# Third layer of a position-bias network: from tiles of eight keys by sixteen sums to tiles of sixteen keys by eight sums

## The chip, the cores and the metric

The kernel runs on one core of a Trainium2 chip. A core has a matrix engine (TensorE, in the profile PE, its weight loads PEld), a vector engine (VectorE, DVE), a scalar engine (ScalarE, ACT), GpSimd (POOL), a queue for transfers (SyncE, SP) and 16 DMA engines. The metric is the device time of one execution in microseconds.

## What is computed

A transformer-like block with deformable attention, followed by a plain attention block. The part that matters here is the bias that is added to the attention logits of the first block. For each of 16 groups (2 images, 8 heads) there are 1024 queries and 64 sampled keys, and each pair of query and key goes through a small network with 128 hidden channels:

```python
pos = grid_q[:, :, None, :] - grid_kv[:, None, :, :]
bias = jnp.sign(pos) * jnp.log1p(jnp.abs(pos))
bias = jax.nn.relu(bias @ cpb_w1 + cpb_b1)     # 2 -> 128
bias = jax.nn.relu(bias @ cpb_w2 + cpb_b2)     # 128 -> 128
bias = (bias @ cpb_w3 + cpb_b3)                # 128 -> 1
sim = jnp.einsum('bhid,bhjd->bhij', qh, kh) + bias
attn = jax.nn.softmax(sim, axis=-1)
```

All data is float32.

## The kernel before

The bias network is a loop of 256 steps (`for s in range(NS)`): 16 groups times 16 steps, each step with 4 keys and all 1024 queries. In one step:

- **Layer 1** (`st_layer1`, L612, VectorE): one instruction adds a table over x and a table over y and clips at zero; the result `h1` has 128 hidden channels on the partitions and 4096 columns. There are three buffers of `h1`, and the step s writes that of step s + 2.
- **Layer 2** (`st_layer2`, L629, TensorE): for each of four blocks z of 32 output channels, eight matmuls of 512 columns. The four keys go to four column groups of the array, so that a PSUM tile has partition 32 * key + lane, and two banks for the two halves of the queries. ScalarE evicts each block with the rectifier (L636 for z = 0 and 2 into `rx`, L638 for z = 1 and 3, with a scale).
- **The third layer's sum over 128 channels** is made in parts. Block 0 is multiplied by its weights and added to block 1 (`st_sum(s, 0)`, L646, VectorE); likewise block 2 to block 3 (`st_sum(s, 2)`). Then GpSimd issues a DMA that adds the second result onto the first one (L648). So each key has 32 lanes left. The weights of block 1 and 3 are taken into the eviction, which works because the channels are ordered by the sign of their weight (`rank`, `order`, `arrange`, once at the start): a "bound" block may hold only channels whose sign fits its place.
- **Folding of lanes.** For a pair of steps s and s + 1 (s even), `st_fold` adds the odd lanes of tile s onto its even lanes (L660, a DMA with accumulation from GpSimd, 64 partitions). `st_join` copies the odd lanes of tile s + 1 to the odd lanes of tile s (L663, SP), and then adds the even lanes of s + 1 there (L665, GpSimd). Tile s then holds 8 keys, each with 16 sums.
- **Layer 3** (`st_layer3`, L694, TensorE) takes two such tiles every four steps: four matmuls of 512 columns with 32 output rows (two halves of the queries, two tiles), which sum 16 lanes for each of 8 keys and put them in their rows of the logits in PSUM (`sims`). The weights `w3f` are zeros with a mask of signs inside; a slice of it moves the result to the right rows. The last four steps of all are taken apart, unfolded, with `w3u`. For each pair of heads `st_layer3` also starts the product of queries and keys (L678).

Buffers of the results: `ua` (4) for even steps, `uo` (2) for odd ones, `ub` (3) for the second sums, `rx` (3).

Beside the loop run, one piece a step, the preparation of later groups (`later`: `chain` for queries and offsets, `sample` for keys and values) and the softmax of finished groups (`softmax_steps`). The order on each engine is that of the program, moved in places by `issue_after`, which puts an instruction behind a given one of its engine. `chain` loads the input rows `xn` and multiplies them with `wq`; `sample` builds interpolation weights `wt` and multiplies the sampled keys with `wk`. `wq` and `wk` lie together in the tile `ws`.

After the loop follow the output projection (L874), the MLP (L927) and the second attention (L1058, L1156).

Of the kernel before, what the change touches and what calls it, by code (L numbers as in the profile page):

```python
# [8 lines left out]
F32 = mybir.dt.float32  # L9
AF = mybir.ActivationFunctionType  # L10
# [36 lines left out]
def conv_seq_kernel(ctx: ExitStack, tc: tile.TileContext, x, xt, kst, pst, cst, vec, wsm, outw, w1, w2, wl, wlt, brow, out):  # L47
# [22 lines left out]
    w3f = cp.tile([P, 56], F32, name="w3f")  # L70
# [70 lines left out]
    with tc.tile_pool(name="lp", bufs=2) as lp:  # L141
# [21 lines left out]
        ws = ph.tile([P, 1408], F32, name="ws")  # L163
        wq, wk = ws[:, 0:512], ws[:, 512:1024]
        pw = [ws[:, 1024 + 128 * i : 1152 + 128 * i] for i in range(3)]
        wv = sx.rearrange("p a f j -> p (a f j)")[:, 0:512]
        ow_s = vp[:, 0:NCH, :]
        nc.scalar.dma_start(out=ws[:, 0:P], in_=wsm[:, 0:P])
# [5 lines left out]
        nc.scalar.dma_start(out=ws[:, 1024:1408], in_=wsm[:, 1536:1920])  # L174
# [4 lines left out]
        def load(b, k):  # L179
            xn = ph.tile([P, HW], F32, name="xn")  # L180
            nc.sync.dma_start(out=xn, in_=xv[:, k, b, :])
            return xn

        xn0 = [load(0, 0)]
# [13 lines left out]
        w2t, crow, tri, four, chan, mask = (  # L198
            pz[:, a:b] for a, b in ((0, 128), (128, 256), (256, 384), (384, 400), (400, 401), (401, 413))
        )  # L200
        wb = vs[:, VOFF["w3"] : VOFF["w3"] + 2]
        po_, rn, t4, pc, dc, k16, one = (
            pw_[:, a:b] for a, b in ((0, 1), (1, 3), (3, 4), (4, 5), (5, 6), (8, 24), (128, 256))
# [15 lines left out]
        def order():  # L219
            nc.vector.tensor_scalar(k16, four, rn[:, 1:2], 4.0, ALU.is_le, ALU.mult)  # L220
            nc.vector.tensor_reduce(t4, k16, AX.X, ALU.add)
            free, bound = ([t.rearrange("p (a b l) -> p b a l", a=2, b=2)[:, i] for t in (place, crow)] for i in (0, 1))
            nc.vector.tensor_scalar(bound[0], bound[1], t4, 64.0, ALU.is_ge, ALU.mult)
            nc.vector.tensor_tensor(bound[0], bound[0], bound[1], ALU.add)
            nc.vector.tensor_scalar(free[0], free[1], t4, None, ALU.add)
            nc.vector.tensor_scalar(perm, place, pc, None, ALU.is_equal)

        def arrange():
            nc.gpsimd.memset(prod, 0.0)
            ps = simp.tile([P, 512], F32, name="sim")  # L230
            nc.tensor.matmul(ps[:, 0:P], w2t, perm, start=True, stop=True)
            for z in range(4):
                for u in range(4):
                    nc.tensor.matmul(
                        ps[32 * u : 32 * u + 32, P + 2 * z : P + 2 * z + 2], perm[:, 32 * z : 32 * z + 32], wb,
                        start=True, stop=True,
                    )
            nc.scalar.copy(cw2, ps[:, 0:P])
            nc.scalar.copy(
                sc[:, 0:8].rearrange("p (a z) -> p z a", a=2), ps[:, P : P + 8].rearrange("p (z a) -> p z a", a=2)  # L240
            )
            nc.gpsimd.tensor_scalar(sc[:, 8:9], sc[:, 1:2], 0.0, 2.0, ALU.is_ge, ALU.mult)
            nc.gpsimd.tensor_scalar(sc[:, 8:9], sc[:, 8:9], 1.0, None, ALU.subtract)
            nc.gpsimd.tensor_scalar(sc[:, 0:4], sc[:, 0:4], sc[:, 8:9], None, ALU.mult)
            for z in (1, 3):
                nc.gpsimd.tensor_tensor(sc[:, 4 + z : 5 + z], sc[:, 4 + z : 5 + z], sc[:, z : z + 1], ALU.mult)
            nc.gpsimd.tensor_scalar(w3f[:, 24:32], mask[:, 0:8], sc[:, 8:9], None, ALU.mult)
            nc.gpsimd.tensor_scalar(w3u[:, 28:32], mask[:, 8:12], sc[:, 8:9], None, ALU.mult)
# [7 lines left out]
        def chain(ci):  # L256
# [3 lines left out]
            for i in range(K):  # L260
                k = k0 + i
                if i == 0:
                    xn = xn0.pop()
                nc.scalar.activation(xn, xn, AF.Identity, bias=col("bn1b", k), scale=bns[:, k : k + 1])
                if ci > 0:
                    yield
                ps = flat("psq")

                for f_, h_, f, h in QUADS:
                    nc.tensor.matmul(  # L270
                        ps[h_, f * 512 : (f + 1) * 512], wq[f_, k * P + 64 * f : k * P + 64 * f + 64],
                        xn[f_, h * 512 : (h + 1) * 512], start=True, stop=True,
                    )
                for f_, h_, f, h in QUADS:
                    copy = nc.vector.tensor_copy if ci == 0 and f == 1 else nc.scalar.copy
                    copy(qa[f_, b, k, h * 512 : (h + 1) * 512], ps[h_, f * 512 : (f + 1) * 512])
                if i + 1 < K:
                    xn = load(b, k + 1)
                elif ci + 1 < len(CHAINS):
                    xn0.append(load(*CHAINS[ci + 1][0]))  # L280
                yield
# [132 lines left out]
        def sample(ci):  # L414
# [23 lines left out]
            for i, (b, k) in enumerate(G):  # L438
# [3 lines left out]
                wt = ph.tile([P, 8, 2, J], F32, name="wt")  # L442
# [10 lines left out]
                for f in range(2):  # L453
                    r, v = slice(64 * f, 64 * f + 64), sg[:, 4, f, i * J : (i + 1) * J]
                    nc.scalar.activation(
                        uv[r].rearrange(rowwise, e=2, t=8), v[r].rearrange(natural, e=2, t=8), AF.Copy,
                        scale=col("bn1b", k)[r],
                    )
# [6 lines left out]
                for t in range(8):  # L465
# [6 lines left out]
                    kv.rearrange(rowwise, e=2, t=8), ps[:, 0:J].rearrange(natural, e=2, t=8), AF.Copy,  # L472
                    scale=bns[:, k : k + 1],
                )
                nc.vector.tensor_tensor(kv, kv, uv, ALU.add)
                yield
# [3 lines left out]
                nc.tensor.matmul(pk[:, 0:J], wk[:, k * P : (k + 1) * P], kv, start=True, stop=True)  # L480
# [38 lines left out]
        with tc.issue_after(nc.cur_bb.bb.instructions[-1]):  # L519
            nc.sync.dma_start(out=wv, in_=wsm[:, 1024:1536])  # L520
            nc.sync.dma_start(out=ow_s, in_=outw)
            nc.sync.dma_start(out=ws[:, P:1024], in_=wsm[:, P:1024])
# [99 lines left out]
        def st_layer2(s):  # L622
            h1 = h1s.pop(s)
            r = []
            for z in range(4):
# [7 lines left out]
                name, bufs = (("rx", 3), (("ua", 4), ("uo", 2))[s % 2], ("rx", 3), ("ub", 3))[z]  # L633
# [18 lines left out]

        def lanes(s, i):
            return sums[s][1].rearrange("(l e) h n -> l e (h n)", e=2)[:, i]

        def st_fold(s):
            with tc.issue_after(added[0]):
                nc.gpsimd.dma_start(out=lanes(s, 0), in_=lanes(s, 1), accum_op=ALU.add)  # L660

        def st_join(s):
            nc.sync.dma_start(out=lanes(s, 1), in_=lanes(s + 1, 1))  # L663
            with tc.issue_after(added[0]):
                nc.gpsimd.dma_start(out=lanes(s, 1), in_=lanes(s + 1, 0), accum_op=ALU.add)  # L665


        def st_layer3(s):
            gi, i = divmod(s // 4, NSL // 4)
# [3 lines left out]
            if f == 0 and i == NSL // 4 - 1:  # L673

                assert state[chain_of[b, k][0]] is None
                sims[gi + 1] = simp.tile([P, 512], F32, name="sim")
                for f_, h_, o, h in QUADS:
                    nc.tensor.matmul(  # L678
                        sims[gi + o][h_, :], kz[f_, b * NCH + k, :], qa[f_, b, k, h * 512 : (h + 1) * 512],
                        start=(o == 1), stop=False,  # L680
                    )
            w = w3f[:, 24 - 8 * i : 56 - 8 * i]
            parts = [[(w, sums[s + 2 * e][1])] for e in range(2)]
            if s + 4 == NS:

                w = [w3u[:, 28 - 8 * i - 4 * o : 60 - 8 * i - 4 * o] for o in range(2)]
                parts = [[(w[o], sums[s + 2 * e + o][1]) for o in range(2)] for e in range(2)]
                parts[1].append((w[1], sums[s + 3][3]))
            for m in range(len(parts[1])):
                for h in range(2):  # L690
                    for e in range(2):
                        if m < len(parts[e]):
# [3 lines left out]
                                stop=(i == NSL // 4 - 1 and m == len(parts[e]) - 1),  # L696
                            )
            for o in range(4):
                sums.pop(s + o)
# [63 lines left out]
        for s in range(NS):  # L763
# [4 lines left out]
            if s % 2 == 1 and 3 <= s < NS - 1:  # L768
                st_join(s - 3)
            if s % 4 == 0 and s // 4 + 1 < 4 * NG:  # L770
                load_tables(s // 4 + 1)
# [33 lines left out]
            if s % 4 == 3 and s >= 7:  # L805
                st_layer3(s - 7)
                if (s - 3) % NSL == 0:
                    tails.append(softmax_steps(s // NSL - 1))
        st_sum(NS - 1, 2)
        st_layer3(NS - 4)  # L810
# [434 lines left out]
def _order(np):  # L1245
# [4 lines left out]
    place = np.where(z % 2 == 1, 4 * (l // 2) + l % 2 + 2 * (z // 2), 32 * (z // 2) + l)  # L1250
    crow = np.broadcast_to(place, (P, P))
    tri = d[:, None] < d[None, :]
    four = np.broadcast_to(4 * np.arange(1, 17), (P, 16))
    pair = (4 * (d % 2) + d // 32)[:, None] == np.arange(8)
    alone = (d // 32)[:, None] == np.arange(4)
    return np.concatenate([crow, tri, four, d[:, None], pair, alone], axis=1).astype(np.float32)
# [87 lines left out]
```

## Time and profile before

| what | us |
|---|---|
| runs of the kernel (three) | 2674.56, 2674.84, 2682.71; median 2674.84 |
| the profiled execution | 2672.5 |
| its span, first to last instruction | 2670.7 |
| start of the first layer-2 matmul | 37.7 |
| end of the last layer-3 matmul | 1922.8 |
| layer 2 on TensorE (L629) | 1784.8 busy |
| layer 1 on VectorE (L612) | 1131.4 busy, 4.40 each |
| sums on VectorE (L646) | 327.0 + 163.5 + 163.6 busy, 1.28 each |

A group row of the profile names the line, the engine, the operation, the tile written and those read, the shapes, how many instructions there are, their busy time, the mean time of one, and the idle time of the engine just before them with what ended it. One matmul of float32 shows as two records. Records of matmuls that run beside each other in different column groups overlap, so the busy time of a group of matmuls is best read from the starts of the next group. A row of the timeline has the start, the length, the engine, the line, the operation, the tiles, how many instructions were merged, and in brackets the idle time before it with what ended it. For DMAs the rows of issues have the queue that issued them, how many, how many KB each and the median time from issue to landing.

### The profile page before, as it was taken

The page shows a single profiled execution, that of the slowest core. Times are in us where ns is not written, and L with a number is a line of the kernel's source. Part 1 is how long each engine was busy: PE and PEld are TensorE (multiplying, and loading weights), DVE is VectorE, ACT ScalarE, POOL GpSimd, SP SyncE. Part 2 cuts the span into 40 slices and gives each one's busy share as a digit, 9 for nine tenths or more (in the row PEclk, how much of TensorE's full clock was granted, in tenths as well). Part 3 has the DMA queues.
Part 4 walks back from the last instruction along what each step waited for, and adds up shares of the span by engine and source line. Part 5 has one row for each costly group of instructions (what it writes and reads, how often), then busy time and mean ns, then how long its engine had stood idle before and what let it go on. Part 6 is the DMA issues. An engine that isn't in the chain of part 4 may idle for free.

```text
span 2670.7 us, 46906 instructions
## 1 busy us (share of the span) xinstructions
PE 2654.7 (99%) x19596; PEld 959.0 (36%) x19596; DVE 2243.1 (84%) x1329; ACT 1690.1 (63%) x2201; POOL 575.5 (22%) x615
## 2 busy tenths in 40 slices
PE   9999999999999999999999999999999999999999
PEld 3343322332333333333323323333344444446455
DVE  7999999999999899999999999999774484466354
ACT  5787898788878888877777777777621131114041
POOL 1222222222222222222222222222243232000000
PEclk9999999999999999999999999999999999999999
DMA  5766766767666666776777676767631111000000
GB/s 199 152 150 144 164 138 142 160 144 157 147 147 151 155 144 141 145 153 140 148 148 145 150 149 143 152 146 148 160 112 47 47 48 45 3 16 0 32 0 32
DMA packets 96131, 316.67 MB, mean 119 GB/s; under 512 B 17104, under 2 KB 19424, under 8 KB 93232
## 3 DMA queue, kind: packets, MB, share of 16 engines
q0 software_dynamic: 57312, 202.26, 40.7%
q1 hardware_dynamic: 38176, 111.10, 11.7%
q8 instruction: 155, 2.54, 0.4%
q14 instruction: 56, 0.46, 0.0%
q10 hardware_dynamic: 432, 0.31, 0.0%
HBM read 74.28 MB, written 6.55 MB: 30 GB/s over the span
## 4 chain that ended last, share of the span: by engine, by line
PE 84%; DMA 5%; issue 4%; DVE 4%; ACT 2%; POOL 1%; DVEq 0%; SPq 0%; POOLq 0%; ACTq 0%
PE ps L629 53%; PE sw L927 14%; PE sw L1058 9%; DMA ua<-ua 2%; DMA ua<-uo 2%; PE sw L1156 2%; PE sim L694 2%; DVE h L612 1%; PE psg L531 1%; DVE ub L646 1%; PE sw L874 1%; ACT rx L636 0%; POOL ua L665 0%; DVE xs L882 0%; DVE ua L646 0%
## 5 line engine op out<-in xcount | busy, mean ns | idle before, releaser
L629 PE MATMUL ps<-h,cw 128*32 128x512 f32 x16384 | 1784.8, 592 | 1.7 <-ACT rx L636 1.6
L612 DVE CUSTOM_DVE_ANT_1 h<-ta,tb 128x4096 f32<-128x4096 f32 (+1 forms) x257 | 1131.4, 4403 | 45.2 <-PE ps L629 41.3
L629 PEld LDWEIGHTS ps<-h,cw 128*32 128x32 f32 x16384 | 541.1, 110 | 1210.6 <-issue 1155.0
L636 ACT ACTIVATE rx<-ps,sc 128x1024 f32<-128x1024 f32 x512 | 568.6, 1111 | 170.5 <-PE ps L629 144.4
L638 ACT ACTIVATE ub<-ps,sc 128x1024 f32<-128x1024 f32 x256 | 308.4, 1205 | 88.5 <-PE ps L629 88.1
L646 DVE SCALAR_TENSOR_TENSOR ub<-rx,sc,ub 128x1024 f32<-128x1024 f32 x256 | 327.0, 1277 | 5.7 <-ACT ub L638 5.7
L648 POOL DMA_DIRECT2D ua<-ub x128 | 114.8, 897 | 722.6 <-DVE ub L646 685.0
L927 PE MATMUL sw<-xb,w1t 128*128 128x512 f32 x448 | 193.7, 592 | 3.0 <-DVE xs L123 3.0
L927 PE MATMUL sw<-hm,w2t 128*128 128x512 f32 x448 | 193.6, 592 | 0.0
L665 POOL DMA_DIRECT2D ua<-uo x126 | 109.8, 871 | 371.3 <-DMA ua<-uo 364.2
L648 POOL DMA_DIRECT2D uo<-ub x127 | 116.4, 916 | 335.8 <-DVE ub L646 283.0
L638 ACT ACTIVATE ua<-ps,sc 128x1024 f32<-128x1024 f32 x128 | 154.2, 1205 | 54.5 <-PE ps L629 54.2
L638 ACT ACTIVATE uo<-ps,sc 128x1024 f32<-128x1024 f32 x128 | 154.1, 1204 | 49.7 <-PE ps L629 43.7
L646 DVE SCALAR_TENSOR_TENSOR ua<-rx,sc,ua 128x1024 f32<-128x1024 f32 x128 | 163.5, 1278 | 12.8 <-ACT ua L638 12.7
L646 DVE SCALAR_TENSOR_TENSOR uo<-rx,sc,uo 128x1024 f32<-128x1024 f32 x128 | 163.6, 1278 | 7.7 <-ACT uo L638 7.3
L123 DVE TENSOR_TENSOR hm<-hm,sw 128x1024 f32<-128x1024 f32 x56 | 67.6, 1219 | 105.1 <-PE sw L927 104.7
L660 POOL DMA_DIRECT2D ua<-ua x126 | 152.1, 1207 | 1.7 <-issue 1.6
L927 PEld LDWEIGHTS sw<-xb,w1t 128*128 128x128 f32 x448 | 85.0, 190 | 110.5 <-issue 105.0
L936 ACT ACTIVATE hm<-hm,vs 128x512 f32<-128x512 f32 x64 | 42.6, 713 | 129.5 <-DVE hm L123 129.5
L927 PEld LDWEIGHTS sw<-hm,w2t 128*128 128x128 f32 x448 | 85.1, 190 | 107.1 <-issue 106.2
L123 DVE TENSOR_TENSOR xs<-xs,sw 128x1024 f32<-128x1024 f32 (+1 forms) x48 | 55.6, 1171 | 72.9 <-PE sw L1058 36.0
L1058 PE MATMUL sw<-aT,vt 128*128 128x512 f32 x224 | 96.7, 593 | 0.3 <-ACT aT L1138 0.3
(239 smaller groups left out, 1798.2 us busy)
## 6 DMA issues: line engine op xcount, KB each, us to landing
ua<-ub POOLq DMA_DIRECT2D x128, 512.0 KB, 4.9
uo<-ub POOLq DMA_DIRECT2D x127, 512.0 KB, 5.3
fb<-fdr SPq DMA_DIRECT2D x64, 512.0 KB, 5.3
ua<-ua POOLq DMA_DIRECT2D x126, 256.0 KB, 6.5
ua<-uo SPq DMA_DIRECT2D x126, 256.0 KB, 2.7
ua<-uo POOLq DMA_DIRECT2D x126, 256.0 KB, 3.8
w1t<-in_w SPq DMA_DIRECT2D x8, 1024.0 KB, 4.8
w2t<-in_w SPq DMA_DIRECT2D x8, 1024.0 KB, 4.8
```

Source lines behind the costliest of these rows:

```text
L123: nc.vector.tensor_tensor(out, a, b_, op)
L612: nc.vector._custom_dve(TENSOR_ADD_SAT, out=h1[:, y : y + step].rearrange("p y t x -> p (y t x)"), in0=a.unsqueeze(1).to_broadcast([P, ste ...
L629: nc.tensor.matmul(ps[32 * q : 32 * q + 32, h, :], cw2[:, 32 * z : 32 * z + 32], h1[:, 16 * h : 16 * h + 16, q, :], start=True, stop=True,)
L636: nc.scalar.activation(o, ps, AF.Relu, bias=sc[:, 4 + z : 5 + z])
L638: nc.scalar.activation(o, ps, AF.Relu, bias=sc[:, 4 + z : 5 + z], scale=sc[:, z : z + 1])
L646: nc.vector.scalar_tensor_tensor(r[1], r[0], sc[:, z : z + 1], r[1], ALU.mult, ALU.add)
L648: nc.gpsimd.dma_start(out=sums[s][1], in_=sums[s][3], accum_op=ALU.add)
L660: nc.gpsimd.dma_start(out=lanes(s, 0), in_=lanes(s, 1), accum_op=ALU.add)
L665: nc.gpsimd.dma_start(out=lanes(s, 1), in_=lanes(s + 1, 0), accum_op=ALU.add)
L694: nc.tensor.matmul(sims[gi][q : q + 32, :], w_, t[:, h, :], start=(i == 0 and f == 0), stop=(i == NSL // 4 - 1 and m == len(parts[e]) - 1),)
L927: nc.tensor.matmul(ps[:, m, :], w[:, a, k, m * P : (m + 1) * P], x[:, b_, k, :], start=(k == 0), stop=(k == 1),)
L1058: nc.tensor.matmul(ps[:, m, :], w[:, a, k, c + m * P : c + (m + 1) * P], x[b_][:, k, :], start=(k == 0), stop=(k == nk - 1),)
```

## The change

Lanes are folded once more. After `st_join`, tile s (s a multiple of 2) has in partition 4l + 2a + e a sum of step s + e. `st_fold2` (for s a multiple of 4) adds the partitions with a = 1 onto those with a = 0, in two DMAs of 32 partitions (e = 0 and 1). `st_join2` copies the partitions with a = 1 of tile s + 2 to those of tile s, in two copies from SP, and adds the partitions with a = 0 of tile s + 2 there, in two DMAs with accumulation from GpSimd. Tile s then holds 16 keys, each with 8 sums, and layer 3 takes two such tiles every eight steps. The channels are ordered in groups of eight by sign in place of four. The last four steps of all stay unfolded and are taken one after another. Results of steps with s % 4 == 2 get buffers of their own (`uc`, 2).

To make room, `wq` and `wk` are no longer held in whole: a piece of 128 columns is loaded with each `xn` and each `xnt`, and `wt` shares the buffer of `xn`, so that the next chain's `xn` is loaded at the end of `sample`.

```diff
-    w3f = cp.tile([P, 56], F32, name="w3f")
+    w3f = cp.tile([P, 48], F32, name="w3f")
...
-        ws = ph.tile([P, 1408], F32, name="ws")
-        wq, wk = ws[:, 0:512], ws[:, 512:1024]
+        ws = ph.tile([P, 3 * P], F32, name="ws")
...
+        wq0 = ph.tile([P, P], F32, name="wq")
+        nc.scalar.dma_start(out=wq0, in_=wsm[:, 0:P])
...
-        def load(b, k):
+        def load(b, k, wq=None):
             xn = ph.tile([P, HW], F32, name="xn")
             nc.sync.dma_start(out=xn, in_=xv[:, k, b, :])
-            return xn
+            if wq is None:
+                wq = ph.tile([P, P], F32, name="wq")
+                nc.sync.dma_start(out=wq, in_=wsm[:, k * P : k * P + P])
+            return xn, wq
...
-            nc.vector.tensor_scalar(k16, four, rn[:, 1:2], 4.0, ALU.is_le, ALU.mult)
-            nc.vector.tensor_reduce(t4, k16, AX.X, ALU.add)
+            nc.vector.tensor_scalar(k8, eight, rn[:, 1:2], 8.0, ALU.is_le, ALU.mult)
+            nc.vector.tensor_reduce(t8, k8, AX.X, ALU.add)
...
-                    xn = load(b, k + 1)
-                elif ci + 1 < len(CHAINS):
-                    xn0.append(load(*CHAINS[ci + 1][0]))
+                    xn, wq = load(b, k + 1)
...
-                wt = ph.tile([P, 8, 2, J], F32, name="wt")
+                wk = ph.tile([P, P], F32, name="wk")
+                nc.sync.dma_start(out=wk, in_=wsm[:, 512 + k * P : 512 + k * P + P])
+                wt = ph.tile([P, 8, 2, J], F32, tag="xn", name="wt")
...
                 nc.vector.tensor_tensor(kv, kv, uv, ALU.add)
+                if i + 1 == K and ci + 1 < len(CHAINS):
+                    xn0.append(load(*CHAINS[ci + 1][0]))
...
-            nc.sync.dma_start(out=ws[:, P:1024], in_=wsm[:, P:1024])
...
-                name, bufs = (("rx", 3), (("ua", 4), ("uo", 2))[s % 2], ("rx", 3), ("ub", 3))[z]
+                name, bufs = (
+                    ("rx", 3), (("ua", 4), ("uo", 2), ("uc", 2), ("uo", 2))[s % 4], ("rx", 3), ("ub", 3)
+                )[z]
...
+        def twos(s, i):
+            t = sums[s][1].rearrange("(l a e) h n -> l a e (h n)", a=2, e=2)[:, i]
+            return [t[:, e] for e in range(2)]
...
+        def add(out, in_):
+            with tc.issue_after(added[0]):
+                nc.gpsimd.dma_start(out=out, in_=in_, accum_op=ALU.add)
+            added[0] = nc.cur_bb.bb.instructions[-1]
...
+        def st_fold2(s):
+            for o, i in zip(twos(s, 0), twos(s, 1)):
+                add(o, i)
+
+        def st_join2(s):
+            for o, i in zip(twos(s, 1), twos(s + 2, 1)):
+                nc.sync.dma_start(out=o, in_=i)
+            for o, i in zip(twos(s, 1), twos(s + 2, 0)):
+                add(o, i)
...
-            w = w3f[:, 24 - 8 * i : 56 - 8 * i]
-            parts = [[(w, sums[s + 2 * e][1])] for e in range(2)]
-            if s + 4 == NS:
-
-                w = [w3u[:, 28 - 8 * i - 4 * o : 60 - 8 * i - 4 * o] for o in range(2)]
-                parts = [[(w[o], sums[s + 2 * e + o][1]) for o in range(2)] for e in range(2)]
-                parts[1].append((w[1], sums[s + 3][3]))
+            w = w3f[:, 16 - 16 * i : 48 - 16 * i]
+            parts = [[(w, sums[s + 4 * e][1])] for e in range(2)]
+            if s + 8 == NS:
+
+                w = [w3u[:, 28 - 16 * i - 4 * o : 60 - 16 * i - 4 * o] for o in range(4)]
+                parts[1] = [(w[o], sums[s + 4 + o][1]) for o in range(4)]
+                parts[1].append((w[3], sums[s + 7][3]))
+                parts[0] = 4 * [None] + parts[0]
...
+            if s % 4 == 0 and s >= 4:
+                st_fold2(s - 4)
+            if s % 4 == 2 and s >= 6:
+                st_join2(s - 6)
...
-            if s % 4 == 3 and s >= 7:
-                st_layer3(s - 7)
-                if (s - 3) % NSL == 0:
+            if s % 8 == 4 and s >= 12:
+                st_layer3(s - 12)
+                if s % NSL == 4:
                     tails.append(softmax_steps(s // NSL - 1))
         st_sum(NS - 1, 2)
-        st_layer3(NS - 4)
+        st_layer3(NS - 8)
```

## The prediction

> **What bounds the kernel now.** I read the engine totals first, then busy time in stretches of sixteen steps of the main loop, then the timeline around one step. The totals:
>
> ```profile
> span 2670.7 us, 46906 instructions
> ...
> PE 2654.7 (99%) x19596; PEld 959.0 (36%) x19596; DVE 2243.1 (84%) x1329; ACT 1690.1 (63%) x2201; POOL 575.5 (22%) x615
> ...
> L694 PE MATMUL sim<-ua,w3f 128*32 128x512 f32 x504 | 74.4, 595 | 1.2 <-DMA ua<-uo 1.2
> ```
>
> TensorE is busy 99% of the span. That alone proves little (matmul ends are modelled), so I looked for gaps. In a quiet stretch one step's 64 layer-2 records start every 6.87 us (0.43 us per four, which run beside each other in four column groups), and nothing but other matmuls lengthens a step. The third layer is such a lengthening: a step with it takes 7.73 us. The row's 74.4 us overlaps other records, so I take its price from starts. TensorE's timeline, first in the loop, then at its end:
>
> ```profile
> 1687.90 1.04 PE L694 MATMUL sim<-ua,w3f 128*32 128x512 f32 x8
> 1688.76 11.77 PE L629 MATMUL ps<-h,cw 128*32 128x512 f32 x108
> ...
> 1918.70 1.04 PE L694 MATMUL sim<-ua,w3f 128*32 128x512 f32 x8
> 1919.56 1.08 PE L694 MATMUL sim<-ua,w3u 128*32 128x512 f32 x8
> 1920.41 1.08 PE L694 MATMUL sim<-uo,w3u 128*32 128x512 f32 x8
> 1921.80 1.05 PE L694 MATMUL sim<-ub,w3u 128*32 128x512 f32 x4 [0.31 <-DVE ub L646]
> 1922.78 3.70 PE L874 MATMUL sw<-qa,vp 128*128 128x512 f32 x8
> ```
>
> One pass of eight records holds TensorE for 1688.76 - 1687.90 = 0.86 us. A pass with only two of the four column groups (x4) is no shorter, 0.98 us.
>
> VectorE is next. Busy time in stretches of sixteen steps (columns: stretch, length, then PE, PEld, DVE, ACT, POOL, clock, DMA share, GB/s):
>
> ```profile
> 394.20:512.10 117.90, 117.23 (x1092) 35.45 (x1088) 117.90 (x69) 99.49 (x138) 28.09 (x32) 1.00 0.68 144
> ...
> 989.90:1106.00 116.10, 115.52 (x1080) 35.70 (x1076) 116.00 (x68) 98.78 (x132) 27.56 (x31) 1.00 0.67 144
> ...
> 1573.10:1688.80 115.70, 115.70 (x1080) 35.22 (x1076) 109.40 (x50) 86.16 (x99) 27.96 (x32) 1.00 0.70 149
> ```
>
> In the last one VectorE has 6.3 us to spare; in the first it has none. Five of the sixteen stretches have it at 99% or more (158, 394, 635, 752 and 990 us): those where the background work reduces taps and prepares samples.
>
> **What the change removes.** Layer 3 ran in the loop at s = 7, 11, ... 255, 63 times; it will run at s = 12, 20, ... 252, 31 times, with the same four matmuls a time. The last of the 63 is the one at 1918.70, so 62 - 31 = 31 passes go before the tail: 31 x 0.86 = 26.7 us. In the tail the passes from 1918.70 to 1922.78 (4.1 us) become five (four last steps, then the last step's second half beside the tile of s = 248): 5 x 0.86 = 4.3 us; the last sum, done at 1921.74, is not late for the fifth. So 26.7 - 0.2, rounded to **26.4 us** off TensorE.
>
> **What it adds: transfers.** Every four steps: two accumulates (fold2) and two copies with two accumulates (join2), each of 32 partitions, 128 KB. That is 252 issues on GpSimd and 126 on SP. By the rows
>
> ```profile
> ua<-ub POOLq DMA_DIRECT2D x128, 512.0 KB, 4.9
> ...
> ua<-ua POOLq DMA_DIRECT2D x126, 256.0 KB, 6.5
> ua<-uo SPq DMA_DIRECT2D x126, 256.0 KB, 2.7
> ua<-uo POOLq DMA_DIRECT2D x126, 256.0 KB, 3.8
> ```
>
> an accumulate of 128 KB, on the line through 4.9 us (512 KB) and 3.8 us (256 KB), lands in 3.25 us, later where it queues behind another (the 6.5 of ua<-ua does). GpSimd's issue of one is 0.84 to 1.2 us (rows L665, L660), so four add about 3.8 us in four steps of 28 us, where it is a quarter busy. The software queue's 57312 packets take 40.7% of 16 engines: 303 ns each; 8064 more packets there and 4032 at the hardware queue's 131 ns make 186 us of all 16 engines over the loop's 1874 us: DMA share 0.70 to **0.80**. Not a bound, but landings may stretch.
>
> A rule of the Trainium skill speaks against such pieces ("SBUF — State Buffer", sections on the port swizzle and the setup-cost knee): use 128 partitions in the largest transfer, because each one pays some 2 us whatever its size, and 32 adjacent partitions reach only 8 of 16 ports. By its fit a piece takes 2.0 + 0.3 = 2.3 us, by my rows 3.25; fold2, copy and add in turn are 6.9 us by the rule, some 8.8 by the rows. Either is latency beside 28 us, and the ports are no matter by the page's own formula: each piece takes every fourth partition of all 128, which touches all sixteen. I take the rows.
>
> **Does the longer chain arrive in time?** GpSimd's timeline in the quiet stretch:
>
> ```profile
> 1678.62 0.84 POOL L665 DMA_DIRECT2D ua<-uo  x1 [4.27 <-DMA ua<-uo]
> 1680.33 0.89 POOL L648 DMA_DIRECT2D uo<-ub  x1 [0.86 <-DVE ub L646]
> 1680.90 1.19 POOL L660 DMA_DIRECT2D ua<-ua  x1
> 1687.20 0.89 POOL L648 DMA_DIRECT2D ua<-ub  x1 [5.10 <-DVE ub L646]
> 1688.97 0.84 POOL L665 DMA_DIRECT2D ua<-uo  x1 [0.89 <-DMA ua<-uo]
> 1694.06 0.89 POOL L648 DMA_DIRECT2D uo<-ub  x1 [4.25 <-DVE ub L646]
> 1694.63 1.19 POOL L660 DMA_DIRECT2D ua<-ua  x1
> ```
>
> The join issued at 1678.62 lands at 1682.4. Fold2 fits the hole 1682.4 to 1687.2 (two issues, 1.8 us). The next join lands at 1692.5; join2's copies go then (2.3 to 4 us), its two adds at 1695.8, behind the fold of 1694.63, and land at about 1703. Layer 3, today at 1687.90 for this tile, moves three steps later, to about 1709. So the tile is there some **6 us** early, as today (at 1687.90 against 1682.4: 5.5). Behind waiting adds on GpSimd stand the next step's accumulates; they release the ub buffers, read again two steps on, so a delay of 2 us is covered by about 9. Behind SP's waiting copies stand the table load and the next join copy, both with holes of over 2 us. The new buffers are no tighter: uc is rewritten eight steps later, ua now sixteen; uo stays at four. Cost of the chain: from 0 to 46 us (each of 31 tiles late by 1.5 us). Today TensorE waits 2.9 us in all for DMA at layer 3; I take **+1 us** more. If the cover is gone, each us late costs 31.
>
> **VectorE.** It keeps its work. In its five full stretches two of four passes go, 1.72 us each, 8.6 us together. If it can't fall further behind, all of that is lost there; if it can, nothing. In the stretch at 394 its sums start up to 9.3 us after their input (3.1 in quiet ones) while TensorE still starts steps 6.87 us apart, so some room is left: half, **+4.3 us**.
>
> **The rest.** wt shares xn's buffer, so the next chain's xn is loaded only after the sample's last matmuls: these end at 105.5, 288.8, 572.8 and 877.0, the load takes 7.1, and xn is read at 122.7, 306.0, 592.0 and 894.2, at least 10 us later. The second chunk of a pair is tighter already (load at 313.2, read at 321.3): 0 to 3 us, taken at 0. wk and wq come in 64 KB pieces a step or more ahead. At the start, 448 KB and one xn fewer travel between 10 and 20 us, but TensorE is full of the weights' products until 37.68: nothing. The ordering by eight is the same few instructions on small tiles.
>
> **Sum.** -26.4 + 1.0 + 4.3 = -21.1 us. The profiled execution took 2672.5 us (span 2670.7 and 1.8 around): 2651.4. The median shown is 2.3 above it: **2654 us**.
>
> **Rivals.**
> - *All of it* (0.15): VectorE takes up the slack everywhere. For: it lags by up to 9 us today without stopping TensorE. Against: it shows no idle time at 394. 2674.8 - 26.4 = 2648.
> - *Nothing measurable* (0.10): the tiles are on average 0.6 us late and VectorE costs as above: 2674.8 - 26.4 + 4.3 + 18.6 = 2671. For: slack today runs from 2 to 9 us, and landings stretch with the share of 0.80.
> - *Slower* (0.13): the two transfers of a pair go one behind the other's landing, since they interleave in one tile; the trace has no such pair. Each of the three pairs then adds a landing (2.3 to 3.3 us), 7.5 us in all with the busier rings, and eats the 6 us: late by 1.5 us at the one place where TensorE takes the tile. 2674.8 - 22.1 + 31 x 1.5 = 2699. It decides from a mean wait of 22.1 / 31 = 0.71 us on.
> - That the pass count doesn't halve I exclude: the schedule is written out.
>
> **Chances.** A run can be told from no change at about 0.3%, 8 us. The forecast's own case has 0.62, the others as given. The forecast and "all of it" are faster; a little of the third too: 0.77 faster, 0.10 same, 0.13 slower. For 8 in 10 I reach from 2644 to 2678; the likeliest case alone is 2647 to 2662.
>
> **What would show it.** L694's records near 250 in the loop instead of 504, still 0.86 us a pass; steps of 6.87 us between; idle before L694 for DMA under 5 us; the new transfers landing in 3 to 5 us; DMA share 0.80 in the stretches; VectorE over 99% in more than five of them. Wrong: a layer-3 pass that waits for ua<-ub or ua<-ua over 0.7 us on average, GpSimd's accumulates starting later than 2 us after their sums, or steps longer than 6.87 us with ScalarE waiting for uo.

## The result, and the profile after

The changed kernel takes **2661.08 us** (median of 5 runs, 2659.38 to 2662.96); the kernel before, run beside it, 2674.82 (5 runs, 2673.87 to 2682.71). The ratio is 0.9944, with a 95% interval from 0.9929 to 0.9959: 13.7 us less, where 21 were forecast. The profiled executions took 2660.99 us and, before, 2672.5: 11.5 apart, because the one before lies 2.3 us under its kernel's median and this one at its median.

The page of the changed kernel, its first lines and its queues:

```profile
span 2659.2 us, 46896 instructions
...
PE 2633.2 (99%) x19344; PEld 965.0 (36%) x19344; DVE 2241.3 (84%) x1329; ACT 1687.2 (63%) x2201; POOL 792.3 (30%) x867
...
q0 software_dynamic: 69408, 235.31, 46.9%
```

TensorE has 252 matmul records fewer (19596 before), which are 126 matmuls, and VectorE does what it did. GpSimd's 252 additional instructions are the new accumulates.

Did the passes go, and what did one cost? TensorE's timeline in the quiet stretch, where one step took 6.87 us before:

```profile
1653.64 1.04 PE L719 MATMUL sim<-ua,w3f 128*32 128x512 f32 x8
1654.50 55.12 PE L633 MATMUL ps<-h,cw 128*32 128x512 f32 x512
1709.43 1.04 PE L719 MATMUL sim<-ua,w3f 128*32 128x512 f32 x8
```

Each pass again holds TensorE for 1654.50 - 1653.64 = 0.86 us. The 512 layer-2 records between two passes are eight steps, and 1709.43 - 1654.50 is 54.93 us, 6.87 us a step with nothing else in it. Sixteen steps of that part of the loop took 115.62 us before and 113.90 after: 1.72 less, two passes.

Busy time in the stretches where VectorE was full (columns: stretch, length, PE, PEld, DVE, ACT, POOL, clock, DMA share, GB/s):

```profile
156.00:272.00 116.00, 114.39 (x1069) 34.77 (x1065) 115.19 (x68) 92.15 (x113) 41.74 (x48) 1.00 0.80 171
391.20:509.30 118.10, 116.41 (x1072) 40.26 (x1068) 118.10 (x69) 99.75 (x138) 41.80 (x48) 1.00 0.80 170
...
982.00:1098.00 116.00, 114.81 (x1072) 35.10 (x1064) 115.97 (x69) 97.08 (x127) 39.49 (x46) 1.00 0.79 170
```

In the second and third of these VectorE is still busy throughout, and TensorE is idle for 1.7 and 1.2 us, where it was for 0.7 and 0.6. In the first TensorE is idle for 1.6 us, and VectorE for 0.8. The same sixteen steps, from start to start, in the kernel before, the changed one, and the changed one with a third uo buffer (experiment 1) or with some of VectorE's work left out (experiment 3); one profile each:

| from step | before | after | after, third uo buffer | after, less for VectorE |
|---|---|---|---|---|
| 16 | 115.95 | 115.98 | 114.08 | 113.96 |
| 48 | 117.83 | 118.09 | 117.73 | 115.21 |
| 80 | 116.62 | 115.32 | 115.32 | 115.31 |
| 96 | 117.38 | 118.19 | 118.25 | 116.04 |
| 128 | 116.12 | 115.86 | 115.75 | 113.61 |
| 176 (quiet) | 115.62 | 113.90 | 113.90 | 113.90 |
| 192 (quiet) | 114.46 | 112.75 | 112.74 | 112.74 |

The five full stretches together gained 0.46 us of the 8.6 that ten passes are worth, though the one from step 80 gained 1.3; each quiet one gained its 1.7.

Where TensorE waits in the full stretches is seen in the waits over the whole loop (who waited <- for whom: us in total, times, longest). Before, then after:

```profile
PEld ps L629 <- ACT rx L636: 23.1, 51, 1.5
...
ACT rx L636 <- DVE ub L646: 11.8, 10, 2.3
```

```profile
PEld ps L633 <- ACT rx L642: 39.3, 67, 2.0
...
ACT rx L642 <- DVE ub L652: 16.6, 15, 2.5
...
ACT uo L644 <- DMA ua<-uo: 11.8, 8, 2.1
...
ACT uo L644 <- DMA uc<-uo: 10.9, 8, 2.9
```

On this line TensorE waits for ScalarE to empty a PSUM bank 16 us longer than before. ScalarE in turn waits for two things: for VectorE, which has not yet read an rx buffer, and for a transfer that still reads a uo buffer. The second one is nearly new (3.5 us before, some 23 after), which made it the first suspect.

### The profile page after: what moved, and what is told of

Read it like the earlier page. It is cut to its first block, busy times and chain, and to the rows that moved or that the text cites. A ratio compares the mean times of both kernels' runs of the same rounds, so it can differ in the third digit from the quotient of the medians.

```text
span 2659.2 us, 46896 instructions
## 1 busy us (share of the span) xinstructions
PE 2633.2 (99%) x19344; PEld 965.0 (36%) x19344; DVE 2241.3 (84%) x1329; ACT 1687.2 (63%) x2201; POOL 792.3 (30%) x867
## 3 DMA queue, kind: packets, MB, share of 16 engines
q1 hardware_dynamic: 46240, 128.15, 13.8%
## 4 chain that ended last, share of the span: by engine, by line
PE 60%; DMA 25%; DVE 7%; issue 6%; ACT 1%; POOL 1%; SPq 0%; POOLq 0%; DVEq 0%; ACTq 0%
PE ps L633 31%; PE sw L956 14%; PE sw L1087 9%; DMA uc<-uo 7%; DMA uc<-uc 6%; DMA ua<-uc 4%; DMA uc<-ub 4%; DVE h L616 3%; PE sw L1185 2%; DMA ua<-uo 1%; DVE ub L652 1%; PE psg L535 1%; DMA ua<-ua 1%; PE sim L719 1%; DVE uo L652 1%
## 5 line engine op out<-in xcount | busy, mean ns | idle before, releaser
L633 PEld LDWEIGHTS ps<-h,cw 128*32 128x32 f32 x16384 | 554.7, 110 | 1205.0 <-issue 1114.6
L671 POOL DMA_DIRECT2D ua<-uc x126 | 158.3, 1272 | 299.5 <-DMA ua<-uc 292.5
L671 POOL DMA_DIRECT2D ua<-ua x189 | 225.4, 1336 | 20.2 <-DMA ua<-uo 16.2
L654 POOL DMA_DIRECT2D uo<-ub x127 | 126.8, 998 | 210.8 <-DVE ub L652 200.1
L671 POOL DMA_DIRECT2D uc<-uo x63 | 54.0, 857 | 340.8 <-DMA uc<-uo 340.4
L654 POOL DMA_DIRECT2D ua<-ub x64 | 59.3, 926 | 178.4 <-DVE ub L652 163.4
L596 ACT ACTIVATE ta<-fb,vs 128x512 f32<-128x512 f32 (+1 forms) x65 | 88.5, 1364 | 10.1 <-DMA fb<-fdr 10.1
```

The costliest lines, as they stand in the source:

```text
L596: nc.scalar.activation(ta.rearrange("p j x -> p x j")[:, :, j0:j1], fb[:, 0, :, j0:j1], AF.Identity, bias=col("cb1"), scale=col("w1x"),)
L633: nc.tensor.matmul(ps[32 * q : 32 * q + 32, h, :], cw2[:, 32 * z : 32 * z + 32], h1[:, 16 * h : 16 * h + 16, q, :], start=True, stop=True,)
L654: nc.gpsimd.dma_start(out=sums[s][1], in_=sums[s][3], accum_op=ALU.add)
L671: nc.gpsimd.dma_start(out=out, in_=in_, accum_op=ALU.add)
```

## The experiments

The expectations call run 1 e1, and so on. The theories. **V**: VectorE's own work bounds the full stretches, so passes taken off TensorE there are worth nothing. **B**: the two uo buffers are held too long by the slower transfers, and a third buffer gives the time back. **T**: the added transfers cost it, by queueing or by bandwidth. All comparisons below are of medians and of two spans of the profiled executions: the loop, from the first layer-2 matmul to the start of the last step, and the tail, from there to the last matmul of layer 3.

| run | median us | loop | tail | ScalarE's wait, uo for DMA | rx for VectorE |
|---|---|---|---|---|---|
| before | 2674.82 | 1874.2 | 11.0 | 3.5 | 12.9 |
| after | 2661.08 | 1860.4 | 13.8 | 22.6 | 19.1 |
| 1: third uo buffer | 2659.93 | 1856.7 | 15.4 | 0.6 | 19.4 |
| 2: no fold2, join2 | 2659.33 | 1858.0 | 13.4 | 14.2 | 22.5 |
| 3: less for VectorE | 2650.48 | 1847.8 | 15.3 | 17.8 | 3.5 |
| 4: 1 and 3 | 2649.38 | 1847.2 | 15.4 | 0.0 | 3.7 |
| 5: before, less for VectorE | 2670.91 | 1871.1 | 11.0 | 0.8 | 1.9 |
| 6: 2 and 3 | 2648.53 | 1847.1 | 13.4 | 1.7 | 3.4 |
| 7: reciprocal on ScalarE | 2662.64 | 1856.7 | 15.6 | 40.9 | 8.3 |
| 8: 1, 7 and later adds | 2656.97 | 1851.4 | 13.4 | 0.0 | 6.3 |
| 9: 8 without 7 | 2658.98 | 1858.0 | 13.4 | 0.0 | 18.7 |
| 10: half of the tap sums on GpSimd | 2666.99 | 1862.7 | 15.6 | 25.2 | 22.7 |
| 11: 9 and 10 | 2662.66 | 1860.5 | 13.4 | 0.0 | 23.6 |

### 1. A third uo buffer

```diff
-                    ("rx", 3), (("ua", 4), ("uo", 2), ("uc", 2), ("uo", 2))[s % 4], ("rx", 3), ("ub", 3)
+                    ("rx", 3), (("ua", 4), ("uo", 3), ("uc", 2), ("uo", 3))[s % 4], ("rx", 3), ("ub", 3)
```

(Two small tiles, hx and kv, share other tiles' memory to make room.)

> The changed kernel with a third uo buffer (room made by letting hx share acc's buffer and kv share gof's). Theory 'late joins': ScalarE's eviction into uo waits for the join's landing because the tile of four steps before is still read (22.7 us of such waits in the changed kernel, 3.5 before), and TensorE stops for it; with a third buffer these waits go and 8 to 13 us come back: 2648 to 2653 us. Theory 'VectorE is full': the stretches in which the gain is missing are those where VectorE has no idle time; another buffer changes nothing there: 2658 to 2661 us.

Measured: 2659.93 us (2657.72 to 2660.98). The waits that were aimed at are gone, 22.6 us to 0.6. The time moved by 1.1 us, and the ranges overlap. The waits list of this run:

```profile
PEld ps L633 <- ACT rx L642: 35.6, 60, 2.1
...
ACT rx L642 <- DVE ub L652: 16.8, 14, 2.5
```

TensorE still waits 35.6 us where it waited 39.3. So for the most part B is a symptom: ScalarE reached the uo buffer early and waited there; without that wait it comes to the next full rx buffer instead. The exception is the stretch from step 16, which the third buffer alone shortens from 115.98 to 114.08 us, at least what its two passes are worth. The other profiles agree: with three buffers 114.29 in run 9 and 114.03 in run 11, with two 116.32 in run 10, and 113.96 in run 2, without the added transfers. There the uo wait is a cause too: the third buffer or relief of VectorE (113.96 in run 3), either alone, brings the time back.

### 2. The added transfers left out

```diff
-            if s % 4 == 0 and s >= 4:
-                st_fold2(s - 4)
-            if s % 4 == 2 and s >= 6:
-                st_join2(s - 6)
```

> The changed kernel without the second fold: st_fold2 and st_join2 are left out, layer 3 takes tiles s and s + 4 as they are, so half of the keys' sums are left out of the logits. TensorE has the same passes as in the changed kernel, DMA and GpSimd the load of the kernel before. 'Late joins': the first joins land as early as before, the uo waits fall to some 4 us, 2648 to 2652 us. 'VectorE is full': its work is unchanged, 2658 to 2661 us. If the busier DMA rings alone are to blame, also 2648 to 2652.

Measured: 2659.33 us (2659.15 to 2660.14), 1.75 less than the changed kernel. The share of the DMA engines in the stretch at 391 fell from 0.80 to 0.67, and VectorE stayed busy for all 118.10 us of it. All of the added traffic together therefore costs some 2 us, and since the ranges of the two kernels overlap, that is not told from nothing: T is small. Within the loop this profile is a balance: the stretch from 16 is 2.0 us shorter than after the change and the one from 96 is 2.5 longer (120.72), with a wait of 2.9 us for a uo buffer in it.

### 3. Less work for VectorE

The sums over twelve taps (L334) read one tap instead.

```diff
-                            nc.vector.tensor_reduce(dst, src, AX.X, ALU.add)
+                            nc.vector.tensor_reduce(dst, src[:, :, 0:1], AX.X, ALU.add)
```

> The changed kernel with 20 to 28 us less of VectorE's background work: the reduction over the taps of the offset convolution reads the first tap alone (the other taps are left out). All transfers stay. 'VectorE is full': the full stretches get room, at least the 8 us missing there come back: 2648 to 2653 us. 'Late joins' with a VectorE that is only late and not the bound: the transfers are issued after its sums, so less lateness helps some, 2653 to 2658 us.

Measured: 2650.48 us (2649.31 to 2652.76), 10.6 less. VectorE's busy time fell by 25.9 us, from 2241.3 to 2215.4. Its waits list and the same stretches as above:

```profile
PEld ps L633 <- ACT rx L642: 21.9, 46, 1.7
...
ACT uo L644 <- DMA uc<-uo: 9.6, 8, 3.0
```

```profile
391.20:509.30 118.10, 118.04 (x1100) 35.92 (x1096) 115.02 (x68) 102.47 (x143) 43.58 (x51) 1.00 0.80 172
...
982.00:1098.00 116.00, 116.00 (x1086) 35.95 (x1081) 114.35 (x68) 102.28 (x138) 41.93 (x48) 1.00 0.83 176
```

VectorE now has 3.1 and 1.7 us to spare, TensorE is busy to within 0.1 us, and its wait for ScalarE is 21.9 us, near the 23.1 of the kernel before, although most of the waits for uo are still there (17.8 us). That is V.

### 4 and 6. The others on top of it

> Both edits: third uo buffer and the reduction over one tap. 'VectorE is full' alone: as e3. 'Late joins' alone: as e1 or up to 2 us less. If both bind in turn: less than either, 2644 to 2648 us.

> e3 without st_fold2 and st_join2 (half of the sums left out of the logits as in e2). With room on VectorE the price of the transfers shows by itself: if they cost nothing, 2649 to 2651 us as e3; if late joins hold TensorE as soon as VectorE doesn't, 2645 to 2648.

Run 4 (the edits of 1 and 3): 2649.38 us (4 runs, 2648.59 to 2651.51), 1.1 under run 3. Run 6 (the edits of 2 and 3): 2648.53 (2647.42 to 2649.46), 2.0 under run 3, between the two forecasts and mostly in the tail (15.3 to 13.4); its ratio to the kernel before (0.9901) is inside run 3's interval (0.9896 to 0.9923). Both effects are as small with VectorE relieved as without, so neither was hiding behind VectorE.

### 5. The kernel before with the same relief

Without this run, experiment 3 would only show that less work is faster.

> The kernel before with the same relief of VectorE as e3 (the reduction over the taps reads the first tap alone, the others are left out). If TensorE bounds the kernel before and VectorE only just fits, this gains little: 2671 to 2675 us, and the distance to e3 (2650.5) is 21 to 25 us, near the 26.4 of the passes. If the kernel before was itself held by VectorE in the full stretches, it gains as e3 did: 2664 to 2667, and the distance stays 14 us.

Measured: 2670.91 us (21 runs, 2668.63 to 2672.59; ratio to the kernel before 0.9985, interval 0.9979 to 0.9992). The relief that was worth 10.6 us after the change was worth 3.9 before it. The distance to run 3 is 20.4 us, near the first forecast of 21 to 25 and not the 14 of the second. In the loops: with VectorE relieved in both kernels the change saves 1871.1 - 1847.8 = 23.3 us; as they are, 1874.2 - 1860.4 = 13.8. The 9.5 us between are what relieving VectorE brings back (6.7 by the medians, in which run 3's longer tail counts against it).

### 7. A real relief: the reciprocal on ScalarE

A version that computes everything has to move VectorE's work, not drop it. Its reciprocal (1.73 us, once per chain) can be had from the logarithm that ScalarE has just taken.

```diff
             nc.scalar.activation(ln, u, AF.Ln)
+            rc = acc.rearrange("p a k y x -> p (a k y x)")[0:64, 0:n]
+            nc.scalar.activation(rc, ln, AF.Exp, scale=-1.0)
...
-            nc.vector.reciprocal(rc, u)
```

> The changed kernel with one VectorE instruction of each chain (the reciprocal of the logarithm's correction, 1.73 us for a pair of chunks, 0.94 for one) given to ScalarE as exp(-ln): four times in the loop, 6 us of VectorE in three or four of its full stretches. 'VectorE is full': 3 to 6 us come back, 2655 to 2658 us, unless the exponential costs ScalarE a table load of 1.3 us each time. 'VectorE is not the bound': 2660 to 2661.

Measured: 2662.64 us (2661.24 to 2668.41): no gain. VectorE's busy time fell by 6.6 us and ScalarE's waits for it from 19.1 to 8.3, but those for uo rose to 40.9. A line of the view of one source line, ScalarE at the new activation (shortest, median and longest in ns, then first and last start):

```profile
L398 ACT ACT_TABLE_LOAD  x5: 1283/1283/1283, 23.0 to 1065.7; - x5
```

In this program a load of 1.28 us stands between the logarithm and each exponential. In all it is only one load more (19 against 18 in the two traces), since four in the softmax fall away, so the loads are not shown to be what ate the gain. The loop did get 3.7 us shorter in this trace, and the tail 1.9 longer. With two buffers of uo, ScalarE runs into the transfers where it ran into VectorE before, and by the median nothing is left.

### 8 and 9. The third buffer, the reciprocal, and the last tile's adds later

Run 8 joins the edits of 1 and 7 and issues join2's accumulates of the last tile one step later, so that GpSimd does not stand before the last sums:

```diff
         def st_join2(s):
             for o, i in zip(twos(s, 1), twos(s + 2, 1)):
                 nc.sync.dma_start(out=o, in_=i)
+
+        def st_join2_add(s):
             for o, i in zip(twos(s, 1), twos(s + 2, 0)):
                 add(o, i)
...
                 st_join2(s - 6)
+                if s < NS - 2:
+                    st_join2_add(s - 6)
+            if s == NS - 1:
+                st_join2_add(s - 7)
```

> e7's reciprocal on ScalarE, e1's third uo buffer, and for the last tile join2's adds issued a step later, behind the accumulate of step 254. 'VectorE is full': e7 less 1 us for the buffer and less up to 1 us at the end of the loop, 2653 to 2657 us.

> e8 without the reciprocal on ScalarE: the third uo buffer, and join2's adds of the last tile behind the accumulate of step 254. If e8 owes its 4 us to these two, 2656 to 2658 us; if the reciprocal had a part, 2658 to 2660.

Run 8: 2656.97 us (2652.94 to 2659.01), ratio 0.9929 (0.9917 to 0.9942). It is the fastest version that leaves nothing out, 4 us under the changed kernel, though the intervals of the two ratios overlap. Run 9, without the reciprocal: 2658.98 (2656.35 to 2661.55). The tail is at 13.4 us in both. In the loops (one profile each) the reciprocal is worth 6.6 us beside three uo buffers (1858.0 to 1851.4) and 3.7 beside two, but the profile of run 8 is that of its fastest execution, 4.0 us under its median. By the medians it is worth 2.0 us beside three buffers, with overlapping ranges, and nothing beside two.

### 10 and 11. Half of the tap sums on GpSimd

GpSimd is idle 70% of the span, so it could add taps 6 to 11 onto 0 to 5 in the last two chains, and VectorE would reduce six taps instead of twelve.

```diff
+                    if ci > 2:
+                        y0, y1 = rows[0][0:2]
+                        lo, hi = (pr[:, t : t + 6, :, y0:y1, :].rearrange("p t k y x -> p t k (y x)") for t in (0, 6))
+                        nc.gpsimd.tensor_tensor(lo, lo, hi, ALU.add)
+                        yield
+                        rows = ((y0, y1, 0, 6), *rows[1:])
```

> The changed kernel, complete, with VectorE relieved in another way than in e3: in the last two chains GpSimd adds taps 6 to 11 to taps 0 to 5, and VectorE reduces six taps in place of twelve, a step later: 8 us less on VectorE, between steps 80 and 150. 'VectorE is full': 3 to 6 us come back there, 2655 to 2658 us. If GpSimd's two microseconds per sum delay the accumulates enough to hold ScalarE, nothing or a loss: 2661 or more.

> e9 and e10 together, complete: 2651 to 2655 us if both gains add up; 2655 to 2658 if the half sum gives nothing.

Run 10: 2666.99 us (7 runs, 2664.21 to 2672.42), 6 us slower than the changed kernel; run 11: 2662.66 (2661.64 to 2667.38), 3.7 slower than run 9 and outside what was expected. The loss was the second forecast of run 10, but not for its reason: in run 11 ScalarE waits for no uo buffer. VectorE's and then GpSimd's timeline around one of the sums in run 10 (start, length):

```profile
727.39 4.41 DVE L622 CUSTOM_DVE_ANT_1 h<-ta,tb 128x4096 f32<-128x4096 f32 x1
731.72 2.64 DVE L658 SCALAR_TENSOR_TENSOR ub<-rx,sc,ub 128x1024 f32<-128x1024 f32 x1
734.28 0.75 DVE L340 TENSOR_REDUCE acc<-prod 128x56 f32<-128x336 f32 x1
```

```profile
729.38 3.90 POOL L328 TENSOR_TENSOR prod<-prod 128x672 f32<-128x672 f32 x1
```

The sum of two tensors that takes VectorE 1.27 us everywhere else takes 2.64 here, and so it does at all four places where GpSimd's sum starts during a layer-1 operation (L622). There the two alternate: GpSimd's sum starts anywhere within the 4.4 us of L622 and always ends 1.48 to 1.49 us after it (here 729.38 + 3.90 = 733.28, against 727.39 + 4.41 = 731.80), and VectorE's next sum ends 1.08 to 1.09 us after GpSimd's. This is what the Trainium skill states ("SBUF — State Buffer", section "Who interferes with whom"): a VectorE instruction with two SBUF inputs and a GpSimd instruction that reads SBUF exclude each other, and the one that comes second is held until the first has ended. A share of bandwidth would have stretched the two together, but L622 keeps its 4.41 us. At the other two sums VectorE waits for the result:

```profile
L340 DVE TENSOR_REDUCE acc<-prod 128x128 f32<-128x768 f32 x2 | 3.1, 1564 | 5.1 <-POOL prod L328 5.1
```

The bill on VectorE: saved 8 x (1.38 - 0.75) + 2 x (2.96 - 1.56) = 7.8 us, paid 4 x 1.37 + 5.1 = 10.6. The net loss of 2.8 us is near what the loops lost (2.3 us, and 2.5 between runs 9 and 11). The rest of run 10's 6 us lies in the tail (13.8 to 15.6) and behind it, where no sum was moved; it was not traced.

## Why the prediction was right, and where its sizes were off

The mechanism was the one forecast: fewer passes on TensorE, a part of it given back on VectorE. The time missed the forecast by 7 us, within the range of 8 in 10 and just inside that of the likeliest case (2662). Part of that nearness is luck. The sum of -21.1 was made for the profiled executions, which are 11.5 apart (the loop 13.8 shorter, the tail 2.7 longer, the start 0.5 earlier); the other 2.2 us come from where the profile before lies in its kernel's runs. Term by term:

- **Removed passes (-26.4).** Right in count and price: 252 + 8 + 4 + 4 + 4 records of layer 3, 0.86 us a pass. In the loop, with VectorE relieved on both sides, 23.3 of the 26.7 us come through.
- **VectorE (+4.3).** This is the term that was mis-sized: "half" of the 8.6 us of the five full stretches. As the kernels are, these gain 0.46 us; with VectorE relieved in both (run 3 against run 5) they gain 7.4. So 6.9 us were held back there and 2.6 beside them, 9.5 in the loop. The 1.9 us of the stretch from 16 are among them and also come back with the third uo buffer, so they are not VectorE's alone. The reason given was that VectorE's lag (9.3 us behind its input at most) left some room. In the changed kernel the lag peaks at 9.2, so none was used. There are three rx buffers, which limit how far ScalarE can run ahead of VectorE; whether a fourth would let the lag grow was not tried. Run 5 shows the same from the other side: the relief gains 3.1 us of loop in the kernel before, so VectorE was stopping TensorE even then. The lag "without stopping TensorE" was too much said: the prediction's own line for the stretch at 394 has TensorE idle for 0.67 us.
- **Transfers (+1).** 1.75 us (run 2) to 2.0 (run 6 against run 3), neither clear of the spread. The DMA share is 0.79 to 0.81 in the five stretches, as worked out, though by luck: 12096 packets more in the software queue, not 8064, at a lower mean (287 ns, where it was 303). That the buffers are "no tighter" did not hold for uo, whose tile is kept until the join has landed: ScalarE's waits for it rose from 3.5 to 22.6 us, one of the prediction's own signs of being wrong, and cost about 1.9 us in the stretch from 16.
- **The tail (0.2 longer).** It cost 2.7 us. The last sum "is not late for the fifth", as forecast: it ends at 1907.51 (start 1906.23, 1.28 us). What was left out is TensorE's order: the fifth pass isn't issued right behind the fourth. Two matmuls (four records) of the next stage stand before it, for 1.91 us, and in run 2, without the last tile's transfers, too.

```profile
1907.39 1.05 PE L719 MATMUL sim<-uo,w3u 128*32 128x512 f32 x4
1908.38 1.98 PE L903 MATMUL sw<-qa,vp 128*128 128x512 f32 x4
1910.29 0.62 PE L719 MATMUL sim<-ub,w3u 128*32 128x512 f32 x1
```

  The matmuls of L903 had to be done anyway, but nothing was won by doing them early: 30 us behind layer 3 TensorE waits 2.76 us for VectorE where it waited 1.01, and from the end of layer 3 to the end of the span it is 747.9 us in both.
- **The chain to layer 3 (6 us early).** It came to 2.1 us in the median, and TensorE's waits for DMAs at layer 3 stay near 2 us in all. The working has a slip: the join at 1678.62 is the second of the two joins of its four steps, not the first. And the tile that decides, that of the later four of each eight steps, has its pass one step later than before, not three. With that put right the sum is much the same (landed at 1682.4, copy by 1686.4, add by 1689.7, pass at 1687.90 + 6.87 = 1694.8: 5 us). What was longer is seen in GpSimd's timeline after the change:

```profile
1696.83 0.85 POOL L671 DMA_DIRECT2D uc<-uo  x1 [7.81 <-DMA uc<-uo]
...
1706.65 0.82 POOL L671 DMA_DIRECT2D ua<-uc  x1 [6.32 <-DMA ua<-uc]
```

  From the join to the second add of join2 it is 9.8 us here and 9.3 in the median, against 3.8 + 2.3 to 4 worked out. The list of DMA issues gives the copies' median landing as 4.6 us. The last add is quick: issued alone, it lands in 2.7 us in the median, between the 2.3 of the rule and the 3.25 of the rows. The pass at 1709.43 starts 2.8 us after its issue, and so just in time.
- **The rest (0).** ScalarE waits 0.6 us in all for the `xn` that is loaded later, and nothing before.
- **The rivals.** "All of it" assumed a lag that can grow; it did not (9.2 us against 9.3). "Nothing measurable" put its loss into late tiles, which cost 2 us. "Slower" needed the two transfers of a pair to go one behind the other's landing. They do go apart, but for another reason: the second copy reads the lanes that the join of the same four steps has still to write, the first doesn't. So only the second is late, and the wait it decides on (0.71 us a pass) was not reached: about 2 us in 31 passes.

Open: of the 3.4 us by which the loop falls short of the removed passes with VectorE relieved, the transfers have 0.7 (run 6); the rest may be VectorE again, which run 3 relieves only in part. That run 8 beats the changed kernel by 4 us is likely, not settled.

## What to carry to other kernels

When the engine that bounds a kernel gets less to do, count the gain by stretches: in those where a second engine is full as well it can be nothing, whatever lag that engine seems to have left. A wait that has grown from 3 to 23 us is not yet a cost; give that buffer one more and see whether the time moves, stretch by stretch: here it was a cost in one of five. To find which of two full engines binds, take work from one of them in both kernels, before and after.

## What was not expected of the hardware

- VectorE's two-input sums and GpSimd's excluded each other to the end of an instruction: 1.27 us became 2.64, four times of four, and GpSimd's own sum waited up to 3.05 us of its 4.53 (run 10). Idle time on GpSimd was not free for VectorE.
- The order in the software queue, more than the size, set the landing: of two 128 KB accumulates of a pair, the one issued behind others landed in 6.7 us in the median, the one issued alone in 2.7.
